# Sixteen graphs through four graph layers: long and short rows sorted as two stages, 32 long-row gathers a graph, and the first dense part ahead of the adjacency load

## The chip, the cores and the metric

The kernel runs on one core of a Trainium2 chip. The metric is the device time of one execution in microseconds (us); lower is better. Times are medians of several executions. The core has these engines, each with an instruction queue of its own that is worked off in order: PE (TensorE, matrix products and transposes), ACT (ScalarE), DVE (VectorE), POOL (GpSimd, which here issues the indirect DMAs, the gathers) and SP (SyncE, which issues the direct DMAs).

## The reference

`x` is 16 x 1024 x 64 float32, `adj` 16 x 1024 x 1024 float32 with few entries per row, more of them in the first rows. Each of four layers takes `h = relu(layernorm(x))` and adds its result to `x`.

```python
# layer 0: gated message passing
m = relu(relu(h @ W1 + b1) @ W2 + b2)
msg = relu(adj @ m)
gi, gh = msg @ W_ih.T + b_ih, h @ W_hh.T + b_hh
r, z = sigmoid(gi_r + gh_r), sigmoid(gi_z + gh_z)
x = x + (1 - z) * tanh(gi_n + r * gh_n) + z * h
# layer 1: normalized adjacency (adj + identity, divided by roots of row sums)
x = x + relu(norm_adj @ (h @ kernel))
# layer 2: quantiles over the neighbours that are left after dilation
kept = dilate(adj > 0)          # every skip-th neighbour of a full row is dropped, both ways
sv = sort(h[neighbours in kept], over the neighbours, channel by channel)
agg = 0.25 * q25(sv) + 0.5 * q50(sv) + 0.25 * q75(sv)     # interpolated
x = x + (relu((h + agg) @ W1 + b1) @ W2 + b2) * mask
# layer 3: mean over neighbours
x = x + ((adj + identity) @ h) / rowsum(adj + identity)
```

Layer 2 is the costly one: for each of 1024 nodes and 64 channels it sorts the values of the node's kept neighbours.

## The kernel before

**Stages.** Each graph b passes eleven stages, which are generators (L1723 to L1815): `fetch` and `load` bring the adjacency in and make strips, transposes and sign matrices; `code`, `rank`, `cut` and `list` count each row's neighbours, rank the rows by length, apply the dilation and write for each ranked row a list of neighbour indices; `mid` is `dense01` (L1288), layers 0 and 1, which ends with the table `tab` in HBM of the features that layer 2 gathers; `gath` gathers them, `sort` sorts, `sums` weighs and adds; `rear` is `dense23` (L1660), the rest of layer 2 and layer 3.

**Rows by rank.** The 128 longest rows are "heavy". Table `HEAVY` (L39) has six classes of (first rank, rows, list length, padded length, kept for the sum, cap). Two rows lie side by side on the partitions as 2 x 64 channels. `idxH` is the flat list of their indices, padded to a multiple of 128, in NCOL columns. `gather_heavy` (L1390) issues two gathers of 128 rows x 64 channels for each column, both into a tile `gh`; four `gh` are there (GH). PE transposes each `gh` into a bank, four to a bank, and ACT copies a bank into its place in the sort buffer `hb0`, whose padding ACT fills with a large number. The other 896 rows are "light", in seven tiles of 128 rows; `gather_light` (L1595) fills `s0` (tiles 1 to 3) with 32 gathers and `s1` (tiles 4 to 7) with 22.

**Sorting.** `sort_heavy` (L1536) runs a fixed network of minimum and maximum instructions on DVE from `hb0` to `hb1` and back, then weighs (`wb`), reduces to `agh` and stores to `agg`. `sort_light` (L1609) does the same from `s0` to `o0` and from `s1` to `o1`. `hb1`, `o0` and `o1` share one buffer, tag "other". `sum_light` (L1626) weighs and stores to `agg`. `dense23` then gathers `zz` from `agg` (8 gathers), puts the rows back in their order and goes on.

**What sets the order.** Class `Order` (L191) writes the order out by hand: it holds a clock for each engine, takes estimated durations from `Engine.duration` (L326), and always advances the stage that can start soonest on its engine, ties going to the stage that stands first by a table of priorities (`rear`, `sums`, `gath` first, `sort` last). What it decides is the order in each engine's queue[...]. All instructions of the stages are issued through one helper, so the profile shows L388 for them.

A stage names what it has to wait for with `after(...)`. The lines that bear on the change:

- `gathers` (L1770): waits for `list{b}`, `mid{b}`, `gath{b-1}` and, for its buffer `hb0`, for `heavy{b-2}`; ahead of group g of the light rows for `sum{b-LIGHTBUFS[g]}.g`.
- `sorts` (L1784): waits for all of `sort{b-1}`, then for `gh{b}`; it sorts the long rows and then both groups of the short ones.
- `middle` (L1764): waits for `mid{b-1}` and for `load{b}` before anything of `dense01`.
- `NLIST` (L47): 2172 list places, so 17 columns and 34 gathers of `gh` a graph.

Of the kernel before, what the change touches and what calls it, by code (L numbers as in the profile page):

```python
# [9 lines left out]
F32 = mybir.dt.float32  # L10
# [9 lines left out]
EPS = 1e-5  # L20
STRIP = 1
DEPTH = 5
LIGHTBUFS = (2, 2)
SGN = 2
AM = 3
GH = 4
# [17 lines left out]
    (56, 32, 20, 32, 16, 20),  # L44
    (88, 40, 15, 16, 12, 15),
)
NLIST = sum(c[1] // 2 * c[2] for c in HEAVY)  # L47
NFLAT = -(-NLIST // P) * P
NSLOT = sum(c[1] // 2 * c[3] for c in HEAVY)
NKEEP = sum(c[1] // 2 * c[4] for c in HEAVY)  # L50
# [343 lines left out]
def kernel(  # L394
# [117 lines left out]
    def lists_for_all():  # L512
# [124 lines left out]
        nc.gpsimd.iota(row, [[1, 1]], base=0, channel_multiplier=1, allow_small_or_imprecise_dtypes=True)  # L637
        step = lc.tile([P, 1], F32, name="step")
        nc.vector.memset(cap[:, 0:1], float(HEAVY[0][5]))
        for c, e in zip(HEAVY, HEAVY[1:]):  # L640
            nc.vector.tensor_scalar(step, row, float(e[0]), float(e[5] - c[5]), ALU.is_ge, ALU.mult)
            nc.vector.tensor_add(cap[:, 0:1], cap[:, 0:1], step)
        for t in range(1, NT):
            nc.vector.memset(cap[:, t : t + 1], float(USED[t] - 1))

# [2 lines left out]
        nc.vector.memset(endm[0:32, SEG_A : SEG_A + 1], 1.0)  # L648
        nc.vector.memset(endm[32:64, SEG_B : SEG_B + 1], 1.0)
        nc.vector.memset(endm[64:128, SEG_C - 1 : SEG_C], 1.0)  # L650

        D = []
        for i in range(DEPTH):
# [344 lines left out]
        def lists(b, S):  # L998
# [84 lines left out]
            V.tensor_copy(fl[:, 9:10], LB[:, SEG_C - 1 : SEG_C])  # L1083
            yield "S", LC
            base = 0
            for ci, (r0, nr, k, _, _, _) in enumerate(HEAVY):
                o = d["idx"][:, base : base + nr // 2 * k].rearrange("h (a k) -> a h k", k=k)
                if ci < 2:
                    kk = k // 8
                    for r in range(nr):  # L1090
                        S_.dma_start(
                            o[r // 2, r % 2].rearrange("(s k) -> s k", s=8),
                            LA[8 * (r0 + r) : 8 * (r0 + r + 1), 0:kk],
                        )
                elif ci == 2:
                    S_.dma_start(o, LC[:, 0:k])
                else:
                    S_.dma_start(o, LH[r0 : r0 + nr, 0:k])
                base += nr // 2 * k
            for t in range(1, NT):  # L1100
                o = OFFS[t] + 1
                ml = ap_.tile([P, P], F32, name="ml", tag="mk", bufs=1)
# [83 lines left out]
        def layernorm_relu(X, h=None, who="m", times=None):  # L1186

            yield "V", X
            s = wp.tile([P, NT], F32, name="ln_s", bufs=2)
            V.reduce_sum(s, X, AX.X)  # L1190
            V.tensor_scalar(s, s, -1.0 / H, None, ALU.mult)
            yield "A", s
            v = wp.tile([P, NT], F32, name="ln_v", bufs=2)
            if h is None:
                h = wp.tile([P, NT, H], F32, name="h" + who, bufs=1)
            for t in range(NT):
                A.activation(h[:, t, :], X[:, t, :], AF.Square, bias=s[:, t : t + 1], accum_out=v[:, t : t + 1])
            A.activation(v, v, AF.Sqrt, bias=eps, scale=1.0 / H)
            yield "V", v
            V.reciprocal(v, v)  # L1200
            if times is not None:
                V.tensor_mul(v, v, times)
            V.tensor_mul(s, s, v)
            yield "A", s, v
            for t in range(NT):
                A.activation(h[:, t, :], X[:, t, :], AF.Relu, bias=s[:, t : t + 1], scale=v[:, t : t + 1])
            return h
# [4 lines left out]
                A.activation(dst[:, t, :], src[:, t, :], func, scale=by[:, t : t + 1])  # L1212

        def t2(name, who="m"):
            return wp.tile([P, NT, H], F32, name=name, tag="t2" + who, bufs=2 if who == "m" else 1)

        def transposed(h, dst):
            for i in range(NH):
# [67 lines left out]
            return pm  # L1286

        def dense01(b, S):  # L1288
            X = wp.tile([P, NT, H], F32, name="X", bufs=2)
            S_.dma_start(X, x[b].rearrange("(t p) h -> p t h", p=P))  # L1290

            h = yield from layernorm_relu(X)
# [4 lines left out]
            pm = yield from product(w1, cat[0:H])  # L1297
            yield from evicted(pm, m1T[0:H], AF.Relu, b1)
            yield "T", m1T
            p2 = yield from bank()  # L1300
            T.matmul(p2, *bias(0), start=True, stop=False)
            ams = streamed(b, 0)
# [41 lines left out]
            A.activation(nn, nn, AF.Tanh)  # L1344
            yield "V", nn

            d0 = t2("d0")
            V.tensor_sub(d0, h, nn)
            V.tensor_mul(d0, d0, rz[:, :, H : 2 * H])
            V.tensor_add(d0, d0, nn)  # L1350
            V.tensor_add(X, X, d0)

            ams = streamed(b, 1)

# [35 lines left out]
        def gather_heavy(b, S):  # L1390

            d = D[b % DEPTH]
            idxH = S["idxH"]
            yield "P", D[b % DEPTH]["tab"], idxH
            S["hb"] = hb = [qp.tile([P, NSLOT], F32, name="hb0", bufs=2), None]
            base = 0
            for _, nr, k, s, _, _ in HEAVY:
                if s > k:
                    f = 2 * (s - k)
                    A.copy(  # L1400
                        hb[0][:, base : base + nr // 2 * s].rearrange("p (a s) -> p a s", s=2 * s)[:, :, 2 * k : 2 * s],
                        pad[:, 0 : nr // 4 * f].rearrange("p (a s) -> p a s", s=f)
                        if nr // 4 * f <= 96
                        else pad[:, 0:f][:, None, :].to_broadcast([P, nr // 4, f]),
                    )
                base += nr // 2 * s
            ghs = {}
            late = 2
            for c in range(NCOL + late):
                if c < NCOL:  # L1410
                    ghs[c] = qp.tile([P, 2, H], F32, name="gh", bufs=GH)
                    for i in range(2):
                        gather(b, ghs[c][:, i, :], idxH[:, i, c : c + 1])
                        yield ("P",)
                c -= late
                if c < 0:
                    continue
                yield "T", ghs[c]
                if c % 4 == 0:
                    pt = yield from bank()  # L1420
                T.transpose(pt[:, c % 4 * P : (c % 4 + 1) * P], ghs[c].rearrange("p i h -> p (i h)"), ident)
                if c % 4 < 3 and c < NCOL - 1:
                    continue
                yield "A", pt
                f0, f1 = c // 4 * 4 * P, (c + 1) * P
                fb = sb = 0
                for _, nr, k, s, _, _ in HEAVY:
                    n = nr // 2
                    lo, hi = max(f0, fb), min(f1, fb + n * k)
                    while lo < hi:  # L1430
                        a, r = divmod(lo - fb, k)
                        m = (hi - lo) // k // 2 if r == 0 and a % 2 == 0 else 0
                        if m:
                            A.copy(
                                hb[0][:, sb + a * s : sb + (a + 2 * m) * s].rearrange(
                                    "p (a s i) -> p a i s", i=2, s=s
                                )[:, :, :, 0:k],
                                pt[:, lo - f0 : lo - f0 + 2 * m * k].rearrange("p (a i s) -> p a i s", i=2, s=k),
                            )
                            lo += 2 * m * k  # L1440
                        else:
                            ln = min(k - r, hi - lo)
                            pair = hb[0][:, sb + a // 2 * 2 * s : sb + (a // 2 + 1) * 2 * s]
# [6 lines left out]
                    sb += n * s  # L1450
                ps1.close(pt)


# [155 lines left out]
        def sort_light(b, S, g):  # L1609
            ts, kept, _ = NETS[g]  # L1610
            n, width = USED[ts[0]], len(ts) * H
            plan = nets[g][0]
            bufs = [S["s", g], qp.tile([P, n * width], F32, name=f"o{g}", tag="other")]
            far(bufs[1], g, 1)

            def view(bf, first, stp, nr, ln, c):
# [147 lines left out]
        def middle(b, S):  # L1764
            if b:
                yield after(f"mid{b - 1}")
            yield after(f"load{b}")
            yield from dense01(b, S)

        def gathers(b, S):  # L1770
            yield after(f"list{b}", f"mid{b}")
            if b:
                yield after(f"gath{b - 1}")
            if b >= 2:
                yield after(f"heavy{b - 2}")
            yield from gather_heavy(b, S)
            yield f"gh{b}"
            for g in range(len(NETS)):
# [4 lines left out]

        def sorts(b, S):  # L1784
            if b:
                yield after(f"sort{b - 1}")
            yield after(f"gh{b}")
            yield from sort_heavy(b, S)
            yield f"heavy{b}"
            for g in range(len(NETS)):  # L1790
                yield after(f"gl{b}.{g}")
                yield from sort_light(b, S, g)
# [14 lines left out]
        for b in range(B):  # L1807
            S = {}
            for name, stage in (
                ("rear", rear), ("mid", middle), ("fetch", fetching), ("load", loads), ("code", coding), ("rank", ranking), ("cut", cutting), ("list", listing),  # L1810
                ("gath", gathers), ("sort", sorts), ("sums", sums),
            ):
                order.add(f"{name}{b}", stage(b, S))
        first = {"rear": 0, "sums": 0, "gath": 0, "conv": 1, "mid": 1, "list": 1, "cut": 1, "rank": 1, "code": 1, "load": 2, "fetch": 2, "sort": 7}
        order.stages.sort(key=lambda q: first[q[0].rstrip("0123456789")])  # L1815
        with tc.manual_schedule():
            order.run()
# [383 lines left out]
```

## Time and profile before

| | us |
|---|---|
| three executions | 2701.03, 2703.5, 2710.99 |
| median | 2703.5 |
| the profiled execution | 2704.4 |
| its span in the profile | 2702.6 |

Busy time in that span:

| engine | us | share | instructions |
|---|---|---|---|
| PE, matmul | 1848.2 | 68% | 8642 |
| DVE | 2269.5 | 84% | 6486 |
| ACT | 1649.8 | 61% | 5060 |
| POOL | 1777.8 | 66% | 1598 |

Three groups of gathers make POOL's time: `s` 864 of 1154 ns, `gh` 544 of 1107 ns, `zz` 128 of 1179 ns. On DVE the largest are the sort of the long rows (`hb` from `hb`, 1072 instructions, 728.2 us, and 256 more, 183.8 us) and of the short ones (`o` from `s` 138.9 us, `s` from `s` and `o` 137.7 us).

Milestones of some graphs (us from the start of the span):

| graph | index list `idxH` ready | first / last `gh` gather | last light gather | sort of long rows | last sum of `rear` |
|---|---|---|---|---|---|
| 0 | 155.2 | 157.2 / 212.2 | 293.6 | 220.9 to 308.3 | 476.5 |
| 3 | 569.8 | 636.5 / 700.7 | 795.8 | 707.7 to 796.2 | 958.1 |
| 8 | 1361.7 | 1409.0 / 1458.2 | 1548.5 | 1509.8 to 1588.5 | 1784.6 |
| 12 | 1930.9 | 1982.1 / 2055.1 | 2129.5 | 2161.5 to 2252.3 | 2404.8 |
| 15 | 2427.4 | 2434.8 / 2498.2 | 2589.9 | 2543.1 to 2609.5 | 2696.6 |

How to read it: a row is one graph's way through the queues. Where a column of one graph runs into that of the next, an engine is never without work there; where the sort starts well after the last `gh` gather, DVE is behind.

### The profile page before, as it was taken

What the parts mean: (1) busy time and instruction counts of PE and PEld (TensorE: products, weight loads), DVE (VectorE), ACT (ScalarE), POOL (GpSimd) and SP (SyncE); (2) the same over time, 40 slices, a digit from 0 to 9 for tenths busy, and PEclk for the clock granted to TensorE, in tenths of its full rate; (3) what the DMA queues carried; (4) which work ended last, traced back from release to release, by engine and by line L of the source; (5) the groups of instructions that cost most, each with busy time, mean ns of one, the idle gap of its engine ahead of it and who ended that gap; (6) DMA issues with size and microseconds to landing.
All of it is one profiled execution on the core that took longest, in us unless ns stands there. A gap on an engine that the chain in (4) does not pass through costs nothing.

```text
span 2702.6 us, 34052 instructions
## 1 busy us (share of the span) xinstructions
PE 1848.2 (68%) x8642; PEld 953.2 (35%) x8642; DVE 2269.5 (84%) x6486; ACT 1649.8 (61%) x5060; POOL 1777.8 (66%) x1598
## 2 busy tenths in 40 slices
PE   5866677757577776868677596768667778623354
PEld 3433343423334334334333343334233443311122
DVE  3438878998989969998986969999589898999991
ACT  7566685775767568485766767666575864522222
POOL 3037357676677878477777767777767767777721
PEclk7868677858788786978878696878778878765667
DMA  6556556655474664667566666557565744422312
GB/s 186 182 143 202 153 150 198 188 148 174 115 238 141 182 192 131 196 168 201 148 184 186 166 186 184 146 152 210 136 208 157 213 126 137 125 66 63 107 51 83
DMA packets 395184, 427.28 MB, mean 158 GB/s; under 512 B 165981, under 2 KB 302755, under 8 KB 394979
## 3 DMA queue, kind: packets, MB, share of 16 engines
q1 hardware_dynamic: 344386, 374.35, 44.4%
q0 software_dynamic: 50592, 50.66, 10.5%
q8 instruction: 72, 1.18, 0.2%
q14 instruction: 134, 1.09, 0.1%
HBM read 340.38 MB, written 84.46 MB: 157 GB/s over the span
## 4 chain that ended last, share of the span: by engine, by line
DVE 37%; PE 21%; POOL 14%; ACT 10%; DMA 9%; issue 8%; SPq 1%; POOLq 0%; DVEq 0%; ACTq 0%
PE bank L388 21%; DVE hb L388 16%; POOL s L388 9%; DVE s L388 5%; DMA am<-adjT 5%; DVE o L388 2%; POOL gh L388 2%; POOL zz L388 2%; ACT hm L388 2%; ACT junk L388 2%; ACT sgn L388 1%; DMA gh<-tab,idxH 1%; DVE ln_s L388 1%; DMA s<-tab,idxL 1%; DVE KH L388 1%
## 5 line engine op out<-in xcount | busy, mean ns | idle before, releaser
L388 POOL DMA_INDIRECT s<-tab,idxL x864 | 997.5, 1154 | 263.4 <-issue 255.5
L388 POOL DMA_INDIRECT gh<-tab,idxH x544 | 602.5, 1107 | 496.2 <-PE bank L388 173.4
L388 DVE TENSOR_TENSOR hb<-hb 128x128 f32<-128x128 f32 (+11 forms) x1072 | 728.2, 715 | 11.2 <-ACT hb L388 3.2
L388 PE MATMUL bank<-am,hr 128*64 128x512 f32 x512 | 269.0, 671 | 79.0 <-ACT hr L388 50.1
L388 PE MATMUL bank<-am,tr 128*64 128x512 f32 x512 | 266.0, 657 | 52.8 <-ACT tr L388 28.0
L388 PE MATMUL bank<-am,m2x 128*65 128x512 f32 x512 | 261.7, 651 | 33.4 <-DMA am<-adjT 29.7
L388 PE MATMUL bank<-ident,a 128*128 128x128 f32 x1024 | 201.7, 344 | 41.0 <-DMA a<-in_adj_dram 13.3
L388 POOL DMA_INDIRECT zz<-agg,posi x128 | 150.9, 1179 | 110.1 <-DMA agg<-s 62.3
L388 ACT ACTIVATE s<-s,wl 128x64 f32<-128x64 f32 x704 | 187.1, 344 | 47.6 <-DVE s L388 47.5
L388 ACT COPY strip<-bank 128x512 f32<-128x512 f32 x256 | 145.3, 587 | 70.0 <-PE bank L388 67.9
L388 DVE TENSOR_TENSOR hb<-hb,hb 128x656 f32<-128x656 f32 (+2 forms) x256 | 183.8, 731 | 3.9
L388 PEld LDWEIGHTS bank<-ident,a 128*128 128x128 f32 x1024 | 151.7, 178 | 81.1 <-issue 28.4
L388 PE MATMUL bank<-ident,gh 128*128 128x128 f32 x272 | 86.2, 343 | 114.5 <-DMA gh<-tab,idxH 92.1
L388 PE MATMUL bank<-ident,zz 128*64 128x128 f32 x256 | 66.5, 351 | 137.4 <-DMA zz<-agg,posi 122.7
L388 PEld LDWEIGHTS bank<-am,hr 128*64 128x64 f32 x512 | 71.7, 153 | 249.5 <-issue 147.2
L388 ACT ACTIVATE sgn<-strip 128x1024 bf16<-128x1024 f32 x128 | 135.2, 1056 | 30.4 <-issue 23.8
L388 ACT ACTIVATE junk<-bank,nkey 128x1024 bf16<-128x1024 f32 x128 | 141.3, 1120 | 6.7 <-PE bank L388 6.6
L388 PE MATMUL bank<-cx,oh 128*128 128x133 f16 (+1 forms) x1280 | 137.1, 254 | 6.4 <-DVE oh L388 6.4
L388 DVE TENSOR_TENSOR o<-s 128x1152 f32<-128x1152 f32 (+2 forms) x192 | 138.9, 752 | 2.2 <-DMA gh<-tab,idxH 0.4
L388 DVE TENSOR_TENSOR s<-s,o 128x576 f32<-128x576 f32 (+5 forms) x256 | 137.7, 548 | 3.3
L388 ACT ACTIVATE g<-bank 64x512 f32<-64x512 f32 x96 | 52.4, 585 | 141.6 <-PE bank L388 141.6
L388 ACT ACTIVATE sgn<-sgn 128x1024 bf16<-128x1024 bf16 x128 | 135.3, 1057 | 4.1
(345 smaller groups left out, 3984.4 us busy)
## 6 DMA issues: line engine op xcount, KB each, us to landing
am<-adjT SPq DMA_DIRECT2D x384, 512.0 KB
a<-in_adj_dram SPq DMA_DIRECT2D x128, 512.0 KB
adjT<-strip SPq DMA_DIRECT2D x128, 512.0 KB
s<-tab,idxL POOLq DMA_INDIRECT x864
gh<-tab,idxH POOLq DMA_INDIRECT x544
wb<-wd SPq DMA_DIRECT2D x32, 198.0 KB
X<-in_x_dram SPq DMA_DIRECT2D x16, 256.0 KB
x<-X SPq DMA_DIRECT2D x16, 256.0 KB
```

Source lines behind the costliest of these rows:

```text
L388: return f(*args, **kw)
```

## The change

Five edits, in the code's order:

1. Table `PARTS` splits the classes of `HEAVY` into (class, first pair, pairs, list length), so that the longer half of a class gets longer lists than the shorter half: 208 and 160 in place of twice 208, 112 and 104, 31 and 24, 20 and 18. 2044 list places, 16 columns, 32 gathers of `gh` a graph in place of 34. Padded lengths in `hb0`, and so the sorting network, stay. The index DMAs of `lists` go by parts, 14 in place of 12 a graph; the padding on ACT is filled from the shortest part's length on.
2. `sorts` ends after the long rows; the short rows are a stage of their own, `smalls`. The long rows of b wait for those of b-1 and `gh{b}`; the short rows of b wait for the short ones of b-1 and their gathers. `o0` and `o1` get a buffer of their own, tag "lighter", apart from `hb1`.
3. `LIGHTBUFS` is (2, 1): one `s1`, so group 1 of graph b is gathered after the sum of group 1 of b-1.
4. In `dense01` the wait for `load{b}` stands after the first part (the load of X, LayerNorm, transposes, first product and its eviction) and no longer ahead of it.
5. Memory for this: one buffer X and one of tag "t2m" in place of two, `d0` computed in place in `h`, `hr` in the buffer of `h2r`.

```diff
-LIGHTBUFS = (2, 2)
+LIGHTBUFS = (2, 1)
+HB = 2
...
-NLIST = sum(c[1] // 2 * c[2] for c in HEAVY)
+
+PARTS = (
+    (0, 0, 1, 208), (0, 1, 1, 160), (1, 0, 1, 112), (1, 1, 1, 104), (2, 0, 8, 52),
+    (3, 0, 8, 31), (3, 8, 8, 24), (4, 0, 8, 20), (4, 8, 8, 18), (5, 0, 20, 15),
+)
+NLIST = sum(n * k for _, _, n, k in PARTS)
...
-            for ci, (r0, nr, k, _, _, _) in enumerate(HEAVY):
-                o = d["idx"][:, base : base + nr // 2 * k].rearrange("h (a k) -> a h k", k=k)
+            for ci, a0, n, k in PARTS:
+                r0, nr = HEAVY[ci][0] + 2 * a0, 2 * n
+                o = d["idx"][:, base : base + n * k].rearrange("h (a k) -> a h k", k=k)
...
-                h = wp.tile([P, NT, H], F32, name="h" + who, bufs=1)
+                h = wp.tile([P, NT, H], F32, name="h" + who, tag="h2r" if who == "r" else None, bufs=1)
...
-            return wp.tile([P, NT, H], F32, name=name, tag="t2" + who, bufs=2 if who == "m" else 1)
+            return wp.tile([P, NT, H], F32, name=name, tag="t2" + who, bufs=1)
...
-            X = wp.tile([P, NT, H], F32, name="X", bufs=2)
+            X = wp.tile([P, NT, H], F32, name="X", bufs=1)
...
             yield from evicted(pm, m1T[0:H], AF.Relu, b1)
             yield "T", m1T
+            yield after(f"load{b}")
             p2 = yield from bank()
...
-            d0 = t2("d0")
-            V.tensor_sub(d0, h, nn)
-            V.tensor_mul(d0, d0, rz[:, :, H : 2 * H])
-            V.tensor_add(d0, d0, nn)
-            V.tensor_add(X, X, d0)
+            V.tensor_sub(h, h, nn)
+            V.tensor_mul(h, h, rz[:, :, H : 2 * H])
+            V.tensor_add(h, h, nn)
+            V.tensor_add(X, X, h)
...
-            bufs = [S["s", g], qp.tile([P, n * width], F32, name=f"o{g}", tag="other")]
+            bufs = [S["s", g], qp.tile([P, n * width], F32, name=f"o{g}", tag="lighter", bufs=1)]
...
         def middle(b, S):
             if b:
                 yield after(f"mid{b - 1}")
-            yield after(f"load{b}")
             yield from dense01(b, S)
...
         def sorts(b, S):
             if b:
-                yield after(f"sort{b - 1}")
+                yield after(f"heavy{b - 1}")
             yield after(f"gh{b}")
             yield from sort_heavy(b, S)
             yield f"heavy{b}"
+
+        def light_sorts(b, S):
+            if b:
+                yield after(f"smalls{b - 1}")
             for g in range(len(NETS)):
                 yield after(f"gl{b}.{g}")
                 yield from sort_light(b, S, g)
...
-                ("gath", gathers), ("sort", sorts), ("sums", sums),
+                ("gath", gathers), ("sort", sorts), ("smalls", light_sorts), ("sums", sums),
...
-        first = {"rear": 0, "sums": 0, "gath": 0, "conv": 1, "mid": 1, "list": 1, "cut": 1, "rank": 1, "code": 1, "load": 2, "fetch": 2, "sort": 7}
+        first = {"rear": 0, "sums": 0, "gath": 0, "conv": 1, "mid": 1, "list": 1, "cut": 1, "rank": 1, "code": 1, "load": 2, "fetch": 2, "sort": 7, "smalls": 7}
```

More of the change, by code (lines that the diff above doesn't have):

```diff
@@ L639, in lists_for_all @@
         nc.vector.memset(cap[:, 0:1], float(HEAVY[0][5]))
-        for c, e in zip(HEAVY, HEAVY[1:]):
-            nc.vector.tensor_scalar(step, row, float(e[0]), float(e[5] - c[5]), ALU.is_ge, ALU.mult)
-            nc.vector.tensor_add(cap[:, 0:1], cap[:, 0:1], step)
+        longest = [(HEAVY[c][0] + 2 * a, min(k, HEAVY[c][5])) for c, a, _, k in PARTS]
+        for (_, m), (r, n) in zip(longest, longest[1:]):
+            if m != n:
+                nc.vector.tensor_scalar(step, row, float(r), float(n - m), ALU.is_ge, ALU.mult)
+                nc.vector.tensor_add(cap[:, 0:1], cap[:, 0:1], step)
         for t in range(1, NT):
@@ L650, in lists_for_all @@
         nc.vector.memset(endm[64:128, SEG_C - 1 : SEG_C], 1.0)
+        for c, a, _, k in PARTS:
+            if c < 2 and a:
+                r = 8 * HEAVY[c][0]
+                nc.vector.tensor_scalar(
+                    endm[r : r + 32, k // 8 : k // 8 + 1], row[r : r + 32], float(r + 16 * a), None, ALU.is_ge
+                )
         D = []
@@ L1095, in lists @@
                 elif ci == 2:
-                    S_.dma_start(o, LC[:, 0:k])
+                    S_.dma_start(o, LC[2 * a0 : 2 * a0 + nr, 0:k])
                 else:
                     S_.dma_start(o, LH[r0 : r0 + nr, 0:k])
-                base += nr // 2 * k
+                base += n * k
             for t in range(1, NT):
@@ L1394, in gather_heavy @@
             yield "P", D[b % DEPTH]["tab"], idxH
-            S["hb"] = hb = [qp.tile([P, NSLOT], F32, name="hb0", bufs=2), None]
+            S["hb"] = hb = [qp.tile([P, NSLOT], F32, name="hb0", bufs=HB), None]
             base = 0
-            for _, nr, k, s, _, _ in HEAVY:
-                if s > k:
-                    f = 2 * (s - k)
+            first = {}
+            for ci, (_, nr, _, s, _, _) in enumerate(HEAVY):
+                first[ci] = base
+                k = min(q[3] for q in PARTS if q[0] == ci)
+                to = hb[0][:, base : base + nr // 2 * s].rearrange("p (a s) -> p a s", s=2 * s)
+                while k < s:
+                    f = min(2 * (s - k), 96)
                     A.copy(
-                        hb[0][:, base : base + nr // 2 * s].rearrange("p (a s) -> p a s", s=2 * s)[:, :, 2 * k : 2 * s],
+                        to[:, :, 2 * k : 2 * k + f],
                         pad[:, 0 : nr // 4 * f].rearrange("p (a s) -> p a s", s=f)
@@ L1405, in gather_heavy @@
                     )
+                    k += f // 2
                 base += nr // 2 * s
@@ L1425, in gather_heavy @@
                 f0, f1 = c // 4 * 4 * P, (c + 1) * P
-                fb = sb = 0
-                for _, nr, k, s, _, _ in HEAVY:
-                    n = nr // 2
+                fb = 0
+                for ci, a0, n, k in PARTS:
+                    sb, s = first[ci], HEAVY[ci][3]
                     lo, hi = max(f0, fb), min(f1, fb + n * k)
                     while lo < hi:
-                        a, r = divmod(lo - fb, k)
+                        a, r = divmod(lo - fb + a0 * k, k)
                         m = (hi - lo) // k // 2 if r == 0 and a % 2 == 0 else 0
@@ L1449, in gather_heavy @@
                     fb += n * k
-                    sb += n * s
                 ps1.close(pt)
@@ L1773, in gathers @@
                 yield after(f"gath{b - 1}")
-            if b >= 2:
-                yield after(f"heavy{b - 2}")
+            if b >= HB:
+                yield after(f"heavy{b - HB}")
             yield from gather_heavy(b, S)
```

## The prediction, made before the changed kernel ran

> **What bounds the kernel now.** I read the page's busy times first, then the waits of POOL, then the timeline of POOL from graph to graph, then busy time by stretch, and last the waits of DVE and the tail.
>
> The page's slices put DVE (84% busy) ahead of POOL (66%):
>
> ```profile
> DVE  3438878998989969998986969999589898999991
> POOL 3037357676677878477777767777767767777721
> ```
>
> But a busy share leaves out what a gather costs before it starts. The waits of POOL (engine, tile, what it waited for: us in total, times, longest) supply it:
>
> ```profile
> POOL s L388 <- issue: 255.5, 838, 0.3
> POOL gh L388 <- PE bank L388: 173.4, 93, 11.1
> POOL gh L388 <- issue: 125.0, 410, 0.3
> POOL gh L388 <- DVE mx L388: 120.7, 1, 120.7
> POOL zz L388 <- DMA agg<-s: 62.3, 4, 57.6
> POOL zz L388 <- issue: 36.4, 114, 2.0
> POOL gh L388 <- DVE c L388: 38.0, 1, 38.0
> POOL gh L388 <- DVE idxH L388: 18.4, 1, 18.4
> ```
>
> The three issue lines are 0.30 us ahead of each gather, 417 us in all; 1778 busy + 417 is 2195 us, 81% of the span. What is left is the fill (120.7), the bank waits inside the long rows' gathers (173.4), two late lists (38.0 at graph 1, 18.4 at graph 6) and the tail (57.6). So from the end of the fill to the last gather POOL never stops for long, which its timeline shows (start, us, instruction, idle before it and its releaser):
>
> ```profile
> 157.22 1.05 POOL L388 DMA_INDIRECT gh<-tab,idxH  x1 [120.68 <-DVE mx L388]
> ...
> 331.52 1.31 POOL L388 DMA_INDIRECT gh<-tab,idxH  x1 [37.96 <-DVE c L388]
> ...
> 2281.10 0.99 POOL L388 DMA_INDIRECT s<-tab,idxL  x1 [0.30 <-issue]
> 2282.40 0.95 POOL L388 DMA_INDIRECT gh<-tab,idxH  x1 [0.30 <-DMA s<-tab,idxL]
> ```
>
> The first gather of graph 14 starts 0.30 us after the last of graph 13. POOL is the chain from 157 to 2590 us: 2433 us for 16 graphs. DVE is close behind it, as busy time by stretch shows (us, then PE, PEld, DVE, ACT, POOL):
>
> ```profile
> 1510.00:2319.00 809.00, 600.19 (x2771) 304.48 (x2770) 713.50 (x2042) 526.63 (x1641) 582.92 (x517) 0.80 0.60 170
> 2543.00:2703.00 160.00, 67.06 (x221) 33.44 (x221) 101.51 (x191) 39.28 (x150) 45.59 (x38) 0.64 0.25 74
> ```
>
> In the middle DVE has 95 us free of 809, split into short waits for ACT and PE. It runs late: at graph 3 the sort of the long rows starts 7 us after its last gather (707.7 against 700.7), at graph 12 it starts 106 us after (2161.5 against 2055.1). That lag costs nothing until the last graph, and there it is the tail: last gather ends 2589.9, graph 15's long rows are sorted only at 2609.5, then its short rows, the gathers `zz` at 2647, the last sum:
>
> ```profile
> 2609.53 2.62 DVE L388 TENSOR_TENSOR o<-s 128x1152 f32<-128x1152 f32 x2
> ...
> 2695.90 0.69 DVE L388 TENSOR_TENSOR u<-Xr,u 128x512 f32<-128x512 f32 x1 [22.52 <-ACT u L388]
> ```
>
> From the last gather to that sum's end is 107 us, and 6.0 more to the end of the span.
>
> [...]
>
> **The change part by part.**
>
> *32 gathers in place of 34.* 2 x 16 = 32 fewer, each 1.107 + 0.30 us: -45 us on POOL's chain. The bank waits shrink by 2 in 34 of 173.4, -10; two more index DMAs a graph on SP and some 14 more ACT copies a graph stand before the same hand-offs, so I take -8. Sorted widths stay (the classes keep their padded lengths), so DVE's work is the same: with the trace's durations its instructions sum to 2253 us before and 2254 after.
>
> *Sorts as two stages.* Nothing is removed. `o0` and `o1` get a buffer of their own, so in DVE's queue the long rows of graph b+1 may stand before or among the short rows of b. What decides is what else is moved: in the changed order the list of the next graph stands later. From the start of `sort_heavy(b)` to the cast `idxH` of b+1, DVE's queue held (trace durations, us) for b = 0 to 14: before 103, 38, 3, 50, 63, 92, 47, 39, 22, -1, -32, -47, -49, -42, -12; after 96, 62, 78, 85, 81, 103, 24, 96, 55, 54, 38, 15, 109, 44, 99. A negative number means that the list stands ahead of the sort. POOL can pass the end of `gh(b)` and work until it needs that list for 54 light gathers of 1.454 and 8 `zz` of 1.48, 90 us (81 at b = 0). Hand-offs (last gather to sort 8, `idxH` to gather 2) are 10. So POOL stalls at each graph by 10 + f x W - 90, where f is elapsed over busy of that stretch. The formula is tried on before: b = 0 and 5 give 36 and 15 at f = 1.04, measured 38.0 and 18.4, elsewhere nothing. f itself measured 1.07 (110.2 over 103.1), 1.00, 1.00 and 1.04 at b = 0, 3, 4, 5; the 1.07 is inside the fill, the other three together give 1.02, which I take. After: 27, 0, 0, 7, 2, 25, 0, 17, 0, 0, 0, 0, 31, 0, 21 = 130 us, against 57 before. So +73.
>
> *First dense part ahead of the load.* In graph 0 eight ranking passes `junk` on ACT (9.6 us) take 45.5 to 64.0 because the dense part lies among them: up to 9 us to gain. The table of features (154.0) and the list (155.2) end together, so both must move: I take -6, bounds 0 and -9. Elsewhere its LayerNorm, transposes and product stand earlier in DVE's, ACT's and PE's queues and only shift work. Its X load is moved past a load's eight strips on SP; with one X buffer it waits for the store of x1, and the strips queue behind it. Three streamed buffers cover this, taken at 0; DVE waited 9.1 us for X before, in 3 waits. [...]
>
> *One buffer for the second short group.* `s1(b)` must wait for the sum of group 1 of b-1. Between those gathers on POOL stand 32 + 32 + 8 others, over 100 us, and the sum follows the sort by some 20: 0[...]. d0 in place, one `t2m`, `hr` sharing a tag: the same instructions, 0 to +10 for waits between neighbours.
>
> *Tail.* POOL now ends later than the sort of graph 15's long rows, since DVE no longer lags. After the last gather remain sort and sum of group 1 (21), agg store and its landing (6), `zz` (12) and the 39 from 2657.1 to 2696.6: 78 in place of 107.
>
> Sum: last gather 2590 - 6 - 45 + 73 - 8 = 2604; + 78 + 6 = span 2688. The profiled execution took 2704.4 for a span of 2702.6 and the median is 2703.5, so + 0.9: about 2689. I round to **2688**, 0.6% below.
>
> **Rivals.** A change within 0.5% (2690 to 2717) is about what a measurement of this kernel can't tell from none.
>
> - *A, the sum above*, stalls 100 to 158 us: 2659 to 2717. Chance 0.42.
> - *B, the saving is kept.* Light and heavy work fill each other's waits and f falls to 0.9 or less, so stalls stay at 57: 2531 + 78 + 6 + 0.9 = 2616. For: DVE has 12% idle in the middle. Against: f measured near 1, and idle there is round trips which the reordering doesn't shorten. 0.20.
> - *C, slower: the next graph's list becomes POOL's bound.* The place is DVE's queue between the start of the long sort and `idxH`. At f = 1.08 stalls are 174, the last gather ends at 2648 and the time is 2733. It decides from f = 1.06 up (stalls above 158). For: 1.07 was seen at b = 0, and every stalled graph adds 1 us per per cent. Against: 1.00 at two others. 0.25.
> - *D, DVE is the bound.* Carrying both queues forward with trace durations, each hand-off as before, gives -13 to +30 us, middle +8: 2711, no change to be told. 0.13.
> - *It doesn't do what it says:* new lengths too small for some row would send the graph to the slow path. The longest list of these inputs is 143 under a limit of 160 or more, and each class has room; excluded.
>
> **How the numbers follow.** A lies below 2690 with 0.29 of its 0.42. Faster: 0.29 + 0.20 + 0.02 of D = 0.51. Same: 0.13 + 0.09 = 0.22. Slower: 0.25 + 0.02 = 0.27. The range 2630 to 2745 leaves out the better half of B and what C gives beyond f = 1.09.
>
> **What would show it.** 512 `gh` gathers; first gather near 151; waits of POOL for DVE of about 130 at `gh`, at graphs 1, 6, 8, 13 and 15; the long sort starting 8 us after its last gather in most graphs; 78 us from last gather to last sum. B shows as few such waits, C as more than 158 us of them, D as the lag of the long sort growing again. Waits of POOL at `s` for a sum, or of DVE for X above 30 us, would prove my zeros wrong; a first gather still at 157, the fill.

## The result and the profile after

| | before | after |
|---|---|---|
| median of 20 runs each | 2703.76 us | 2690.31 us |
| from, to | 2689.32, 2718.21 | 2672.49, 2706.58 |
| ratio, 95% interval | | 0.9944, 0.9929 to 0.9959 |
| the profiled execution, its span | 2704.4, 2702.6 | 2672.49, 2670.6 |

The change makes the kernel 0.6% faster; the forecast was 2688. The profile of after is of its shortest execution, 18 us under its median, so the parts below explain 32 us where the medians differ by 13. Every account and every wait below is of one execution: a difference of ten or twenty us in one term between two profiles can be chance, since the executions of after alone lie up to 34 us apart.

The page's slices for after, DVE and POOL:

```profile
DVE  3458999898998979898999989789997989989481
POOL 4037468787776877677777877667776647776761
```

The waits of POOL in after (us in total, times, longest):

```profile
POOL gh L394 <- PE bank L394: 138.0, 94, 8.5
POOL gh L394 <- DVE nz L394: 126.7, 1, 126.7
...
POOL gh L394 <- DVE idxH L394: 82.3, 5, 27.3
...
POOL zz L394 <- DMA agg<-s: 22.9, 1, 22.9
POOL zz L394 <- DVE hb L394: 12.9, 1, 12.9
```

Against before, the bank waits fell from 173.4 to 138.0, the late lists rose from 56 us at two graphs (38.0 + 18.4) to 82.3 at five, and the wait for `agg` at the end fell from 57.6 to 22.9. POOL's groups on the pages of before (L388) and after (L394); the figures are count, busy us, mean ns, idle us before them:

```profile
L388 POOL DMA_INDIRECT s<-tab,idxL x864 | 997.5, 1154 | 263.4 <-issue 255.5
L388 POOL DMA_INDIRECT gh<-tab,idxH x544 | 602.5, 1107 | 496.2 <-PE bank L388 173.4
...
L394 POOL DMA_INDIRECT s<-tab,idxL x864 | 1056.7, 1223 | 263.4 <-issue 256.4
L394 POOL DMA_INDIRECT gh<-tab,idxH x512 | 552.5, 1079 | 472.6 <-PE bank L394 138.0
```

There are 32 gathers of `gh` fewer, but each of the 864 of `s` takes 1223 ns in place of 1154: 59 us that were in no part of the prediction. The timeline of POOL at the first gather, at graph 13 and at the end of the gathers:

```profile
159.94 1.11 POOL L394 DMA_INDIRECT gh<-tab,idxH  x1 [126.69 <-DVE nz L394]
...
2152.55 0.95 POOL L394 DMA_INDIRECT gh<-tab,idxH  x1 [27.31 <-DVE idxH L394]
...
2590.97 1.01 POOL L394 DMA_INDIRECT s<-tab,idxL  x1 [0.30 <-issue]
```

and the last sum on DVE's timeline:

```profile
2662.90 0.69 DVE L394 TENSOR_TENSOR u<-Xr,u 128x512 f32<-128x512 f32 x1 [21.96 <-ACT u L394]
```

The last gather ends at 2592.0, where it ended at 2589.9 before. In these two executions POOL comes to its last gather equally late; the whole difference of the two profiles is behind it, 72 us to the last sum in place of 107. The short tail doesn't need the split: it is 68 us in e2 below, the class table alone with one sort stage, and 71 in e3, which joins the sorts again.

An account of POOL from the start of the span to the last gather, from the starts and ends of all gathers (a gap's excess over 0.33 us, which is counted as issue, is put to the gather that it precedes). The terms add up to the last gather whatever sets the time, so that they do so proves nothing by itself:

| us | before | after | difference | in the prediction |
|---|---|---|---|---|
| first gather | 157.2 | 159.9 | +2.7 | -6 |
| `gh` busy | 602.5 | 552.5 | -50.0 | -35 |
| issue | 467.4 | 457.7 | -9.7 | -10 |
| waits inside `gh` | 152.6 | 107.9 | -44.7 | -8 |
| late lists | 55.8 | 80.6 | +24.8 | +73 |
| `s` busy | 997.5 | 1056.7 | +59.2 | 0 |
| waits at `zz` | 13.7 | 37.1 | +23.4 | 0 |
| `zz` busy | 143.3 | 139.6 | -3.7 | 0 |
| last gather | 2589.9 | 2592.0 | +2.0 | +14 |

### The profile page after: what moved, and what is told of

The parts are those of the page before. It is cut to its first block, busy times and chain, and to the rows that moved or that the text cites. A ratio compares the mean times of both kernels' runs of the same rounds, so it can differ in the third digit from the quotient of the medians.

```text
span 2670.6 us, 34077 instructions
## 1 busy us (share of the span) xinstructions
PE 1830.0 (69%) x8626; PEld 951.5 (36%) x8626; DVE 2252.4 (84%) x6494; ACT 1654.4 (62%) x5074; POOL 1783.4 (67%) x1566
## 4 chain that ended last, share of the span: by engine, by line
DVE 26%; PE 21%; POOL 19%; DMA 12%; ACT 12%; issue 9%; SPq 1%; POOLq 0%; DVEq 0%; ACTq 0%
PE bank L394 21%; POOL s L394 12%; DVE hb L394 10%; DMA am<-adjT 5%; POOL gh L394 3%; POOL zz L394 3%; DVE s L394 3%; DMA gh<-tab,idxH 3%; DVE o L394 2%; DMA s<-tab,idxL 2%; ACT sgn L394 2%; ACT s L394 2%; ACT hm L394 1%; SPq L394 1%; ACT junk L394 1%
## 5 line engine op out<-in xcount | busy, mean ns | idle before, releaser
L394 POOL DMA_INDIRECT s<-tab,idxL x864 | 1056.7, 1223 | 263.4 <-issue 256.4
L394 POOL DMA_INDIRECT gh<-tab,idxH x512 | 552.5, 1079 | 472.6 <-PE bank L394 138.0
L394 DVE TENSOR_TENSOR hb<-hb 128x128 f32<-128x128 f32 (+11 forms) x1072 | 727.1, 713 | 24.1 <-ACT hb L394 20.8
L394 PE MATMUL bank<-am,hr 128*64 128x512 f32 x512 | 268.9, 672 | 102.0 <-ACT hr L394 66.6
L394 PE MATMUL bank<-am,tr 128*64 128x512 f32 x512 | 277.6, 685 | 76.7 <-DMA am<-adjT 39.3
L394 PE MATMUL bank<-am,m2x 128*65 128x512 f32 x512 | 258.6, 646 | 17.4 <-DMA am<-adjT 13.8
L394 PE MATMUL bank<-ident,a 128*128 128x128 f32 x1024 | 194.9, 338 | 73.4 <-DMA a<-in_adj_dram 40.5
L394 ACT ACTIVATE s<-s,wl 128x64 f32<-128x64 f32 x704 | 190.0, 351 | 84.6 <-DVE s L394 84.1
L394 POOL DMA_INDIRECT zz<-agg,posi x128 | 147.1, 1150 | 99.0 <-issue 37.9
L394 ACT COPY strip<-bank 128x512 f32<-128x512 f32 x256 | 145.2, 588 | 101.9 <-PE bank L394 88.8
L394 PEld LDWEIGHTS bank<-ident,a 128*128 128x128 f32 x1024 | 147.5, 174 | 119.3 <-issue 48.9
L394 DVE TENSOR_TENSOR hb<-hb,hb 128x656 f32<-128x656 f32 (+2 forms) x256 | 183.9, 731 | 3.7
L394 PEld LDWEIGHTS bank<-am,hr 128*64 128x64 f32 x512 | 72.4, 154 | 268.8 <-issue 153.6
L394 DVE TENSOR_TENSOR o<-s 128x1152 f32<-128x1152 f32 (+2 forms) x192 | 139.7, 752 | 24.6 <-DMA s<-tab,idxL 22.2
L394 PE MATMUL bank<-cx,oh 128*128 128x133 f16 (+1 forms) x1280 | 144.2, 259 | 22.7 <-DVE oh L394 21.1
L394 PEld LDWEIGHTS bank<-am,tr 128*64 128x64 f32 x512 | 72.6, 155 | 227.4 <-issue 142.3
L394 PE MATMUL bank<-ident,gh 128*128 128x128 f32 x256 | 79.6, 340 | 99.6 <-DMA gh<-tab,idxH 95.7
L394 ACT ACTIVATE sgn<-strip 128x1024 bf16<-128x1024 f32 x128 | 135.1, 1055 | 19.7 <-issue 10.6
L394 ACT ACTIVATE g<-bank 64x512 f32<-64x512 f32 x96 | 51.7, 584 | 150.0 <-PE bank L394 149.6
L394 ACT ACTIVATE junk<-bank,nkey 128x1024 bf16<-128x1024 f32 x128 | 141.3, 1114 | 0.4 <-PE bank L394 0.4
L394 DVE TENSOR_TENSOR s<-s,o 128x576 f32<-128x576 f32 (+5 forms) x256 | 138.2, 548 | 2.9
L394 ACT ACTIVATE sgn<-sgn 128x1024 bf16<-128x1024 bf16 x128 | 135.3, 1057 | 4.1
```

The costliest lines, as they stand in the source:

```text
L394: return f(*args, **kw)
```

## The experiments

The theories: P, POOL's chain of gathers and waits for lists sets the end, as the prediction has it; D, DVE's work with its round trips does, whatever the order; some runs have a rival of their own, named in the expectation. Times are medians, each ratio is to the kernel before on the same chip. The bands are those of the expectations, in us; D's are worked out from its per cents.

| kernel | us | ratio | 95% interval | P said | D said |
|---|---|---|---|---|---|
| e1, change without the class table | 2706.42 | 0.9995 | 0.9973 to 1.0017 | 2640 to 2675 | 2682 to 2698 |
| e2, class table alone | 2731.3 | 1.0091 | 1.0055 to 1.0127 | 2690 to 2720 | 2695 to 2711 |
| e3, change without the split | 2715.37 | 1.0037 | 1.0018 to 1.0056 | 2726 or less | 2682 to 2698 |
| e4, change without the early dense part | 2695.57 | 0.9953 | 0.9934 to 0.9973 | 2700 to 2723 | 2682 to 2698 |
| e5, change, list ahead of sorts | 2749.67 | 1.0164 | 1.0145 to 1.0182 | 2610 to 2640 | 2677 to 2703 |
| e6, e1 and list ahead | 2729.83 | 1.0082 | 1.0062 to 1.0102 | e5 + 45 to 53 | e5, within 10 |
| e7, e3 and list ahead | 2727.1 | 1.0070 | 1.0054 to 1.0087 | e5, within 10 | none |
| e8, change, no long sort | 2646.41 | 0.9775 | 0.9751 to 0.9799 | 2290 to 2350 | none |
| e12, change planned with 1.50 us a gather | 2676.88 | 0.9873 | 0.9835 to 0.9911 | 2640 to 2670 | 2677 to 2703 |

P's band holds in e3 alone, where it has no lower end, D's in e4 and, by a fraction of a us, in e12.

**One part undone or done alone.**

e1:

```diff
 PARTS = (
-    (0, 0, 1, 208), (0, 1, 1, 160), (1, 0, 1, 112), (1, 1, 1, 104), (2, 0, 8, 52),
-    (3, 0, 8, 31), (3, 8, 8, 24), (4, 0, 8, 20), (4, 8, 8, 18), (5, 0, 20, 15),
+    (0, 0, 2, 208), (1, 0, 2, 112), (2, 0, 8, 52),
+    (3, 0, 16, 31), (4, 0, 16, 20), (5, 0, 20, 15),
 )
```

> The changed kernel with its class table put back to one list length per class: 2172 places, 34 gathers of gh a graph; the split sorts, the single buffers and the early dense part stay. In this kernel's own DVE queue the work from the start of the long sort of b to the list of b+1 is 97, 47, 45, 60, 21, -8, -9, 19, -2, 6, 27, 6, 45, -6, 7 us for b = 0 to 14, so the formula of the prediction (10 + 1.02 W - 90) gives stalls at late lists of 27 us in place of 130. Theory P (POOL's chain: gathers plus stalls at late lists sets the end): +45 for the gathers, +8 for bank waits, about -100 for stalls if DVE keeps up, at most +29 of tail if it lags again: between 2640 and 2675, faster than before. Theory D (DVE's work is the bound and the order is indifferent): within 0.3% of the changed kernel, 2682 to 2698. Theory G (only the number of gathers counts, stalls stay as in the changed kernel): 2690 + 45 = 2735.

e2 is the kernel before with the class table and what reads it:

```diff
-NLIST = sum(c[1] // 2 * c[2] for c in HEAVY)
+PARTS = (
+    (0, 0, 1, 208), (0, 1, 1, 160), (1, 0, 1, 112), (1, 1, 1, 104), (2, 0, 8, 52),
+    (3, 0, 8, 31), (3, 8, 8, 24), (4, 0, 8, 20), (4, 8, 8, 18), (5, 0, 20, 15),
+)
+NLIST = sum(n * k for _, _, n, k in PARTS)
...
```

> The kernel before with only the class table of the change: 32 gathers of gh a graph, one sort stage, two s1, wait for the load ahead of the first dense part. Work in DVE's queue from the long sort of b to the list of b+1: 107, 64, 9, -36, -3, -8, 94, 98, 63, 100, 97, 82, 69, 40, 57 us, by the formula 116 us of stalls in place of 47. Theory P: -45 - 8 + 69 on POOL's chain, and up to -29 of tail because DVE no longer lags at the end: 2690 to 2720, little or no gain from the saved gathers alone. Theory D: 2703 within 0.3%. Theory G: 2650 to 2658.

e3:

```diff
         def sorts(b, S):
             if b:
-                yield after(f"heavy{b - 1}")
+                yield after(f"smalls{b - 1}")
```

> The changed kernel, except that the long sort of b+1 waits for the short sorts of b, as one stage did; the separate buffers stay. Work from the long sort to the next list: 96, 62, 78, 85, 81, 103, 48, 101, 64, 83, 95, 94, 93, 67, 110 us, by the formula 166 us of stalls in place of 130. Theory P: +36, so 2726, or less by as much as the formula overstates (it gave 130 where the changed kernel's trace has 82 us of waits for idxH). Theory D: 2690 within 0.3%. A rival S (the split itself is what helps, by letting DVE fill waits): the waits of DVE grow and the time goes back to 2703 or above.

e4:

```diff
             yield "T", m1T
-            yield after(f"load{b}")
             p2 = yield from bank()
...
+            yield after(f"load{b}")
             yield from dense01(b, S)
```

> The changed kernel with the wait for the adjacency load put back ahead of the first dense part. Work from the long sort to the next list: 115, 53, 42, 103, 43, 44, 37, 62, 91, 95, 100, 63, 99, 75, 99 us, by the formula 163 us of stalls in place of 130. Theory P: +33 for stalls; the first gather, which came at 159.9 in the changed kernel and at 157.2 before, within 5 us of 157, so the early dense part is worth nothing in the fill: 2700 to 2723. Rival F (the gain of the change is the fill and the earlier dense part): first gather above 165 and 2705 or more. Theory D: 2690 within 0.3%.

e1 misses theory P's 2640 to 2675 by 31 us or more: with 34 gathers its late lists are 61 us, where the formula gave 27. It misses theory D's band too, by 8. e2 is slower than before although it has 32 gathers fewer and nothing else; theory G (2650 to 2658) falls. Its waits of POOL:

```profile
POOL gh L393 <- PE bank L393: 203.0, 103, 15.6
POOL gh L393 <- DVE mx L393: 122.1, 1, 122.1
...
POOL gh L393 <- DVE idxH L393: 76.4, 3, 31.1
...
POOL gh L393 <- DVE hb L393: 29.6, 2, 29.2
```

Its late lists add up to 123 us in the account (56 before, 116 by the formula) and its bank waits to 203. So the saved gathers are spent at late lists, as the prediction said of the change; beyond them the account has 43 us more for `s` (1204 ns a gather) and 17 more bank waits. The table is worth -0.5% on top of the other parts (e1 to after, 16 us) and +0.9% alone. e3 loses 25 us to after. Its account has 112 us of late lists against 81, which P expects, but also 144 us of waits inside `gh` against 108, which P doesn't have; and rival S, with 2703 or more, is met as well, so e3 alone doesn't tell why the split helps. e4 can't be told from after (the intervals overlap), and its first gather is at 160.5: the early dense part does nothing for the fill, so rival F falls. P fails here too: it asked for 2700 or more, and although e4 has 103 us of late lists against 81, it is as fast as after.

**The list ahead of the sorts.** e5 to e7 keep every instruction and change the order:

```diff
                     t = self.start(s[2], s[3])
+                    n = s[0].rstrip("0123456789")
+                    if s[2] == "V" and n in ('sort', 'smalls') and int(s[0][len(n):]) + 1 < 16:
+                        if f"list{int(s[0][len(n):]) + 1}" not in self.done:
+                            t += 3.0
```

> The changed kernel with one more rule where the order is written out: a sort step of graph b on DVE counts as starting 3 us later as long as the list of b+1 isn't written. The same instructions, another order: work from the start of the long sort of b to the list of b+1 is 18, -4, -20, -9, 9, -4, -16, -7, 8, -22, 10, -16, -9, -3, -3 us, so the formula gives no stall at late lists (82 us of waits for idxH in the changed kernel's profile). Theory P (late lists are what POOL's chain loses): the waits for idxH fall under 15 us and the time falls by 50 to 80 us, to 2610 to 2640. Theory D (DVE's work and its round trips are the bound, the lists were late because DVE had no time): the waits fall as well, but the long sorts lag their gathers instead or other waits of POOL grow, and the time stays within 0.5% of 2690.

> The same rule for the order with 34 gathers of gh a graph (one list length per class), the formula gives no stall here either. This prices the two gathers a graph with the lists in time. Theory P: slower than the run beside it, which has 32 gathers and the same rule, by 45 to 53 us. Theory D: within 10 us of it.

> The same rule with the long sort of b+1 again behind the short sorts of b; stalls by the formula none. It prices the split of the sorts with the lists in time. Theory P: within 10 us of the run with the rule and the split, since the split would matter only through when the lists come. Rival S (the split lets DVE fill waits): slower by the 25 us that joining cost without the rule.

The late lists went to 0, 5 and 8 us, and all three became slower. Waits of POOL in e5:

```profile
POOL s L398 <- ACT s L398: 85.1, 3, 44.2
...
POOL s L398 <- DVE oc L398: 33.4, 1, 33.4
...
POOL s L398 <- DVE s L398: 18.0, 1, 18.0
POOL s L398 <- DVE mrc L398: 15.0, 1, 15.0
```

and one of them on the timeline of POOL:

```profile
2051.30 1.23 POOL L398 DMA_INDIRECT s<-tab,idxL  x1 [44.22 <-ACT s L398]
```

Such waits stand before the first gather of the second short group at graphs 1, 2, 5, 6, 9 and 11, 149.5 us in all: the one `s1` is still being sorted and summed. The same wait is 108 us in e6 and 142 in e7, and zero in before and after. So pulling a list ahead pushes the sum of the short rows behind, and with one `s1` POOL pays for that. Between the end of `gh` and the need for the list there is room for 90 us of DVE's work, between that list and the need for `s1` for about as much (an estimate: 64 gathers of 1.4 to 1.5 us, from after's means of 1.079 and 1.223 us and 0.30 of issue); the long sort and the short sorts of a graph have to fit into these two gaps, and in the change's own order they nearly do. D's words ("other waits of POOL grow") fit what happened, its number doesn't: DVE has the same work in e3, e4, e5, e7 and e12 (2249 to 2277 us), and they lie between 2677 and 2750, so the order is not indifferent. In e6 against e5 34 gathers are quicker than 32 by 20 us; their orders differ, in the wait for `s1` by 41 us; the price of a gather with the lists in time was therefore not found. e7, with the sorts joined, beats e5: under this rule the split shows no gain of its own, and rival S, which asked for a loss of 25 us, falls. P, which asked for no difference, misses by 13.

**DVE's largest work taken away.** e8 leaves out the network that sorts the long rows, so it doesn't compute their quantiles; it has two executions, 0.4 us apart.

```diff
-            yield from network(net16, view)
-            cur, p = at16[0], 16
-            ends = {16: cur}
+            cur, p = 0, 256
+            ends = {q: 0 for q in (16, 32, 64, 128, 256)}
             while p < 256:
```

> The changed kernel with the sorting network of the long rows left out: the values of the 128 longest rows are weighed unsorted, so their quantiles are not computed; everything else stays. It takes some 900 us of DVE's work away and shows what POOL's chain is alone. Theory P with the gathers' length set by what DVE does beside them: gathers of gh and s near 1.0 us in place of 1.08 and 1.22, no late lists: 160 fill + 16 x (86 + 8) x 1.3 + bank waits 100 + tail 70 = 2290, up to 2350. If the length of a gather has nothing to do with DVE, they stay at 1.15 and more and the time is 2450 or more.

DVE has 1460 us of work in place of 2252, and the time falls by 44 us only. POOL's groups in e8:

```profile
L394 POOL DMA_INDIRECT s<-tab,idxL x864 | 881.8, 1021 | 263.3 <-issue 258.5
L394 POOL DMA_INDIRECT gh<-tab,idxH x512 | 500.3, 977 | 717.1 <-PE bank L394 260.0
```

and its waits:

```profile
POOL gh L394 <- PE bank L394: 260.0, 120, 10.5
...
POOL gh L394 <- DMA tab<-hm: 106.3, 6, 39.1
...
POOL gh L394 <- DVE mra L394: 24.7, 1, 24.7
POOL gh L394 <- DVE LC L394: 24.6, 1, 24.6
```

The gathers became 250 us shorter (POOL is busy for 1532 us in place of 1783), as theory P said. The 2290 to 2350 didn't come: POOL now waits for PE's banks (260), for the table of features that layers 0 and 1 make (106), for lists. The page of each kernel also follows back the chain of work that ended last, over all engines, by what released each instruction; its shares of the span in before, after and e8:

```profile
DVE 37%; PE 21%; POOL 14%; ACT 10%; DMA 9%; issue 8%; SPq 1%; POOLq 0%; DVEq 0%; ACTq 0%
...
DVE 26%; PE 21%; POOL 19%; DMA 12%; ACT 12%; issue 9%; SPq 1%; POOLq 0%; DVEq 0%; ACTq 0%
...
PE 30%; DVE 24%; ACT 15%; DMA 14%; POOL 10%; issue 6%; SPq 2%; DVEq 0%; ACTq 0%; POOLq 0%
```

So a third chain, with PE's products and the adjacency loads (`am`) in it, stands close behind (PE leads the chain of e8 with 30%, and its waits for `am` are 106.0 us, 88.2 in after); in the order written here it isn't seen to end much before 2646. That DVE lost a third of its work for 1.6% doesn't refute DVE as the bound of after: had DVE set 2690 and the third chain 2646, the same 44 us would have come out. It shows that in this order POOL's shorter gathers and DVE's smaller work together are worth no more than this.

**A better price in the order.** The order is planned with 1.43 us a gather; after's trace has 1.223 + 0.30 for `s`.

```diff
         if self.letter == "P":
-            return 1.43, 0.0
+            return 1.5, 0.0
```

This kernel (e11) and the list-ahead rule on the kernel before, with 32 (e9) and 34 gathers (e10), ran first:

> The kernel before with the class table of the change (32 gathers) and the rule that a sort step of b counts as 3 us later while the list of b+1 isn't written. Here the second short group has its two buffers, so the 150 us in which POOL waited for the one s1 when the rule was put on the changed kernel can't come. Work from the long sort to the next list: 44, -8, -38, -47, -20, 56, 17, 21, -7, -51, -40, -48, -47, -25, 3 us: no late list by the formula, where the same kernel without the rule had 123 us of them and took 2731. Theory P (late lists on POOL's chain): 2731 - 123 = 2608, plus up to 40 of tail because DVE lags: 2608 to 2650. Theory D (DVE's work and its round trips bound all orders alike): DVE lags by 50 us and more at the long sorts, and the time is 2690 to 2720, level with the kernel before.

> The kernel before with the same rule alone: 34 gathers, two s1. Late lists by the formula 0 (56 us in the profile before). Theory P: 2703 - 56 plus nothing in the tail, which already lags: about 2650, and 45 to 53 us slower than the run beside it with 32 gathers. Theory D: 2690 to 2720, and within 10 us of the run beside it.

> The changed kernel, with the duration that the order is planned with for one gather set to 1.50 us in place of 1.43, nearer to what its trace shows (1.223 + 0.30 for s, 1.079 + 0.30 for gh). The same instructions in another order: work from the long sort to the next list 86, 100, 57, 82, 56, 36, 32, 87, 109, 63, 77, 39, 30, 65, 74 us, 80 us of late lists by the formula in place of 130, and the last sum of the second short group comes at most 112 us of DVE's work after the next list, so that its one buffer is free in time in nearly every graph. Theory P: 50 us fewer late lists, 2640 to 2660. Theory D: 2690 within 0.5%.

In that group the kernel before itself took 3509 us, and in the profile of e9 the queue of SP waits 382.3 us, and DVE at `oc` 141.7 us, for events that the profile ties to nothing on the core (none in after). The three results (3489, 3555 and 3328, ratios 0.9989, 1.0160 and 0.9490) decide nothing, and why this group was slow stays open, as does whether early lists pay with two `s1`. e11 was run again as e12:

> The same kernel as the run before it, the changed kernel planned with 1.50 us a gather, since in that run the kernel before took 3509 us in place of 2704 and the times can't be set against the others. Theory P (late lists are what is left to win on POOL's chain, and here the one s1 is free in time): late lists near 50 us in place of 81, no wait at the first gather of s1, 2640 to 2670. Theory D: 2690 within 0.5%, with the waits that vanish at the lists coming back as bank waits inside the gathers of gh or as longer gathers. Theory T (three chains of nearly one length, the queues that feed the adjacency to PE among them, as the run without the long sort's 2646 suggests): no more than 20 us gained, not below 2665.

e12 takes 2676.88, 0.9873 of before; its interval lies below that of after (0.9929 to 0.9959), so it is the fastest kernel that computes everything, though the two didn't run on the same chip. Its waits of POOL:

```profile
POOL gh L394 <- PE bank L394: 152.4, 94, 11.9
POOL gh L394 <- DVE nz L394: 125.7, 1, 125.7
...
POOL gh L394 <- DVE idxH L394: 34.7, 2, 23.1
```

Late lists are 46 us in the account (81 in after), with no wait at `s1`; the gain on after is 13 us by the medians, 19 by the ratios to before on each chip. P's direction holds, its 2640 to 2670 doesn't by the median; theory T's bound of 20 us does. D isn't excluded here: its band just holds, and it said that what vanishes at the lists would come back as bank waits (138.0 to 152.4) and longer gathers (`s` 1223 to 1241 ns), as it did in part.

## Why the prediction was right, point by point

- **POOL carries the end.** Not shown. The last sum comes 67 to 81 us after the last gather in after, e1 to e7 and e12 (107 before, where DVE lagged), but that is 67 us in e8 too, where POOL waits for PE and the feature table. On the page's chain, which the prediction leaves out, DVE leads in before (37%) and in after (26%), ahead of PE (21% in both) and of POOL (14 and 19%). POOL, DVE and PE wait for each other in turn (in after POOL at `gh` 138.0 us for PE's banks, PE 83.0 us for DVE's `agh`, DVE at `o` 22.2 us for the gathers of `s`); which of them sets the time of after stays open.
- **Gathers saved, -45.** Measured -60 (-50 busy, -10 issue): the `gh` gathers that are left also took 28 ns less each. That they can be worth less than nothing alone was not in the text as a case of its own; e2 shows it.
- **Late lists, 130 us.** The mechanism was right: predicted at graphs 1, 4, 5, 6, 8, 13 and 15, found at 1, 6, 8, 13 and 15. The size was not: 81. For graphs 1 and 13 the formula gave 27 and 31, measured were 26.5 and 27.0; for 6, 8 and 15 it gave 25, 17 and 21, measured 10.3, 2.1 and 14.7. The term that was mis-sized is POOL's cover of 90 us, which took a light gather at 1.454 us; at 1.523 it is 94 us, and the formula gives 105. The other 24 us are open.
- **The same formula elsewhere.** As theory P it gave bands for e1 to e8 and e12, and only that of e3 held. With the lists in time (e5) it asked for 2610 to 2640, and 2750 came. It finds graphs at which POOL waits for a list; it doesn't foresee what the kernel does with the time when that wait goes away.
- **Bank waits, -8.** Measured -45 in the account. That these waits would shrink by more than the columns saved was not seen; with 32 gathers they ranged from 88 (e4) to 170 us (e2) over e2 to e5, e7 and e12; why isn't shown.
- **First dense part, -6 and zeros.** Failed: the first gather came 2.7 us later, and e4 shows no effect of the move. The one `s1` cost nothing, as predicted, in the change's own order only. DVE's waits for X were 6.1 us (9.1 before): the zero held.
- **Tail, 78.** Right: measured 72, and DVE no longer lags: its long sort starts 3 to 29 us after its gathers.
- **What was in no term:** `s` gathers +59 and waits at `zz` +23. With the oversized lists (-48) and bank waits (-37) they nearly cancel. That the total came within 2 us of the median is largely luck; the profiled span is 17 us under the forecast one.
- **D** gave 2711. That the order is indifferent is refuted by e5 to e7; DVE's work as one of several chains of nearly one length is not.

## What to carry to other kernels

Where three engines are each as busy as here (DVE 84%, PE 69%, POOL 67% of the span of after), price an edit by the order that it leaves in the queues, not by the instructions that it saves: here the same instructions ran between 2677 and 2750 us. Check each buffer that a change makes single against every other order in use, since it can narrow the window in which two kinds of work must both be done: POOL waited 149.5 us for the one `s1` in e5, not at all in after. And feed measured durations back to whatever writes the order: one such value was worth as much as the whole change, 13 us by the medians. No other value was tried, so whether the better price did it or a lucky order isn't shown.

## What was not expected of the hardware

How long a gather takes goes with what DVE does beside it. Over the profile of before, gathers with DVE idle for at least 80% of their time took 946 ns on average (137 of them), those with DVE at work for at least 80% 1167 ns (1320). It goes with the kind of work too: where DVE's tensor_tensors fill at least 90% of the gather's time it took 1236 ns (654), where DVE is at work for 80% or more but with other instructions (tensor_tensors 10% at most) 980 ns (136). After gives 946, 1271 and 980 for idle, tensor_tensors and others. The longest of after, 6.52 us, on POOL's timeline:

```profile
1348.91 6.52 POOL L394 DMA_INDIRECT s<-tab,idxL  x1 [0.30 <-issue]
1355.73 0.94 POOL L394 DMA_INDIRECT s<-tab,idxL  x1 [0.30 <-issue]
```

and on DVE's at that time:

```profile
1348.29 1.53 DVE L394 TENSOR_TENSOR hb<-hb 128x640 f32<-128x640 f32 x2
...
1349.83 2.61 DVE L394 TENSOR_TENSOR o<-s 128x1152 f32<-128x1152 f32 x2
...
1352.46 1.54 DVE L394 TENSOR_TENSOR hb<-hb 128x640 f32<-128x640 f32 x2
1353.93 0.67 DVE L394 TENSOR_TENSOR X<-X,u 128x512 f32<-128x512 f32 x1
...
1354.80 0.93 DVE L394 TENSOR_TENSOR hb<-hb 128x128 f32<-128x128 f32 x3
```

It lasts through a run of wide tensor_tensors, of 512 to 1152 columns, and ends at 1355.43 among narrow ones, of 128. e8 agrees with the split by instruction: with the long sort left out (792 us less of DVE's work) the means of `gh` and `s` fall from 1079 and 1223 to 977 and 1021 ns. Which gathers are long follows the order: in e5 DVE works at `hb` for 38% of the time of the `gh` gathers (10% in after) and 32% of that of `s` (52%), and `gh` takes 1235 and `s` 1118 ns, in after 1079 and 1223. So the one price that the prediction put on every gather saved, 1.107 + 0.30 us, was wrong as a constant. Why gathers beside tensor_tensors take longer isn't shown; no run changes the instruction alone.
